# A decoder layer on one Trainium2 core: first rows by pairs, the 64-row products first, four shared lower parts behind the experts

## The chip, the cores and the metric

The kernel runs on one core of a Trainium2 chip. The metric is the device time of one execution in microseconds (us). Three runs of the kernel before gave 1570.51 to 1572.54 us, with a median of 1572.47 us. Beside them stands one execution that was recorded by the hardware profiler; every duration below is from it. A change of 0.2% is about 3.1 us.

## The reference, cut to what matters

Input `x` has 4 sequences of 512 rows of 512 numbers, all float32. Three blocks are each added to the running `x`:

```python
x = x + attention(layernorm(x), wq, wk, wv, wo)      # 32 query heads, 8 key/value heads, causal, rope
x = x + block_quantized(layernorm(x)) @ block_quantized(ctx).T
x = x + moe(layernorm(x))
# moe: probs = softmax(h @ Wg); every row goes to its best expert e (8 experts, 256 rows each at most);
#   routed = (silu(h @ W1[e]) * (h @ W3[e])) @ W2[e] * gate      # inner width 704 = 5 * 128 + 64
#   shared = (silu(h @ sw1) * (h @ sw3)) @ sw2                   # for all rows, inner width 704
#   x = x + routed + shared
```

## The kernel before, in words

**Order of work.** Every engine has one in-order stream of instructions, written out by the Python program. TensorE (PE) carries nearly all of the time. The program has four stages.

1. *The start* (lines 152 to 1056). The first sequence's four row tiles `h_0` to `h_3` (128 rows each) and the first weights are loaded. Two queues carry loads: `bulk` is ScalarE's (ACT's) queue, `nc.sync` is SyncE's (SP's). Meanwhile PE runs 52 transposes of the identity, `spin_a` (L169). VectorE (DVE) takes mean and variance of each row tile (`ln_mean_var`, L224 and L225), then an inverse root by an integer guess and three Newton steps on [128 x 4] values (`ln_root`, L238 to L247), then scales the four tiles (`ln_apply`, L251). PE transposes them (`ptr_h`, L257), ACT copies them into `hT` (L299), and PE goes on with the first value projection `psv` (L350; it needs only the first tile's part of `hT`), two transposes of the rope table `prt` (L1048) and the first key projection `psk` (L308; it needs all of `hT`).
2. *Attention.* A planner (`Fill`, with a due time, a cost and a chain of predecessors for each job) puts projections, output projections, the second block and the routing (`job_w`) between the score, transpose and value steps. The change leaves the order of this stage as it is.
3. *The shared expert, beside the last jobs* (`units`, from L1344). I write U(b,c) for `shared_up(b, c)`, the upper part of sequence b and inner chunk c, and D(b,j) for `shared_down(b, j)`, the lower part of the two row tiles j and j+1 of sequence b. Chunks 0 to 4 have 128 inner rows; chunk 5 holds the last 64. Except for b = 0, chunks 0 to 4 are computed by `up7` with seven half-size products instead of eight (L1281); it needs sums of blocks of the input, `xS`, made by `shared_sums(b)`, and of the weights, `wS`, made on GpSimd (POOL) by `weight_sums`. For the last sequence, b = 3, VectorE makes three of the four sums and POOL one. At the end of each chunk POOL multiplies the two halves into `gT` (L273). The order is U(0,0..5) D(0,0) U(1,5) D(0,2), U(1,0..4) D(1,0) U(2,5) D(1,2), U(2,0..4) D(2,0) U(3,5), U(3,0..4). The planner's last jobs run inside D(2,0): there the last sequence's routing product `pc` (L688), and from it, on DVE, the destinations `r_dst_i` (L712). Four indirect DMAs on POOL (L719) then scatter that sequence's rows into `xd`. Expert 0's two row tiles `xe` are read from `xd` by SP (L1397) and transposed on PE (`turn_rows(0)`, `ptr_e`) two units before the end of the stage, ahead of U(3,3).
4. *The experts and the tail.* For e = 0 to 7: five `up7` chunks of expert e (`p_e`), with expert e+1's weight sums on POOL; chunk 5 of expert e+1 (`expert_rest`); then the lower part `epy` (`down`, L1212 and L1222). `down` does two row tiles: for each, chunks 0 to 4 (two passes of a 128-row product each), and then for both the 64-row products of chunk 5 (L1222). Results go by VectorE (L1480) and SP (L1482) to `oe`. Behind expert 7 stand D(2,2), D(3,0) and D(3,2). Sixteen gathers on POOL (L1492) fetch the routed rows, VectorE adds them (`combine`, L1500), and SP writes the output (L1505, or L1341 where a shared lower part is added last). `rows_back` reads rows that had been parked in memory.

PSUM banks come from small rings: four named `sp`, three named `mm`, one `av`. A product that takes the next bank waits until its former content has been read.

Of the kernel before, what the change touches and what calls it, by code (L numbers as in the profile page):

```python
# [23 lines left out]
def decoder_layer(  # L24
# [92 lines left out]
    def tile_v(b):  # L117
        return pj.tile([P, KC, 512], F32, tag="wq", bufs=2, name=f"wv_{b}")

    def load_v(b):  # L120
        w = wts["v0"] if b == 0 else tile_v(b)
        bulk(out=w, in_=wv.rearrange("(k p) n -> p k n", p=P))
        wts["v"] = w

# [25 lines left out]
            issue(out=rows[b, j], in_=xf[i * P : (i + 1) * P, :])  # L150

    load_h(0)
    wts["v0"] = tile_v(0)
    load_v(0)
    load_k(0, 0)

    ident = const.tile([P, P], F32, name="ident")
# [2 lines left out]
    nc.gpsimd.tensor_copy(ident_b, ident)  # L160

    warm = const.tile([P, 1], F32, name="warm")
    nc.scalar.activation(warm, ident[:, 0:1], AF.Exp)

    def spin(n, name):

        pt = bank("sp", f"spin_{name}")
        for j in range(n):
            nc.tensor.transpose(pt[:, 0:P], ident, ident)  # L169

    spin(52, "a")

    mask = am1.tile([P, T], F32, name="mask")
    nc.gpsimd.memset(mask, 0.0)
# [155 lines left out]
    def job_k(b, a):  # L330

        t1 = yield from rotated(b, wts["k", a], 0, f"k_{b}_{a}")
        yield -0.6
        for g in range(2):
            kT = am1.tile([P, T], F32, tag="kT", bufs=4, name=f"kT_{b}_{2 * a + g}")
            for half in range(2):
                bulk(out=kT[half * HD : (half + 1) * HD, :], in_=t1[g * HD : (g + 1) * HD, :])
            kTs[b, 2 * a + g] = kT
# [692 lines left out]
    for _ in job_hs(0):  # L1031
        pass
    rsrc = am1.tile([P, TB, 2, 2, HD], F32, tag="pT", bufs=2, name="rsrc")
    for c in range(2):
        for half in range(2):
# [2 lines left out]
                rsrc[:, :, c, :, half * HH : (half + 1) * HH],  # L1038
                rp[:, :, c, lo : lo + HH].unsqueeze(2).to_broadcast([P, TB, 2, HH]),
            )  # L1040
    for gen in (job_h(0), job_v(0, 0)):
        for _ in gen:
            pass
    rt = pj.tile([P, 2, T], F32, name="rt")
    for c in range(2):
        pt = bank("mm", f"prt_{c}")
        for it in range(TB):
            nc.tensor.transpose(  # L1048
                pt[:, it * P : (it + 1) * P],
                rsrc[:, it, c, :, :].rearrange("p h d -> p (h d)"),  # L1050
                ident,
            )
        nc.scalar.copy(rt[:, c, :], pt)
    for gen in (job_k(0, 0), job_q(0, 0), job_q(0, 1), job_q(0, 2)):
        for _ in gen:
            pass
# [148 lines left out]
    def down(gT, w2, t, name, tag, mid=None):  # L1205

        pys = []
        for i in range(2):
            py = bank(tag, f"{name}_{i}")
            pys.append(py)  # L1210
            for c in range(HF):
                nc.tensor.matmul(  # L1212
                    py,
                    gT[:, c, (t + i) * P : (t + i + 1) * P],
                    w2[:, c, :],
                    start=(c == 0),
                    stop=False,
                )
                if mid and c % 2:
                    mid()  # L1220
        for i, py in enumerate(pys):
            nc.tensor.matmul(  # L1222
                py,
                gT[i * HT : (i + 1) * HT, HF, (t + i) * P : (t + i + 1) * P],
                w2[i * HT : (i + 1) * HT, HF, :],
                start=False,
                stop=True,
            )
        return pys

# [25 lines left out]
    def token_sums(x, ts, cols, vector=False):  # L1256

        half = cols // 2
        b11, b12, b21, b22 = (x[:, k : k + 2, t : t + half] for k in (0, 2) for t in (0, half))
        t1, t2, t3, t4 = ts  # L1260
        us = 1.27 * cols / T
        gpsimd(us, t3, b22, b12, ALU.subtract)
        for out, y, z in (t1, b12, b11), (t2, b22, t1), (t4, b21, t2):
            if vector:
                nc.vector.tensor_tensor(out, y, z, ALU.subtract)
            else:
                gpsimd(us, out, y, z, ALU.subtract)
        return t1, t2, t3, t4, b11, b21, b22
# [41 lines left out]
    def shared_up(b, c, mid=None):  # L1310
        if b not in gTs:
            gTs[b] = gp.tile([P, NHC, T], F32, tag="gT", bufs=2, name=f"gT_{b}")
        if b and c < HF:
            up7(se["w"][0], xS[b], gTs[b][:, c, :], c, T, f"s{b}_{c}", mid)
        else:
            up(se["w"][0], h3x[b], gTs[b], c, T, f"s{b}_{c}", mid)
        if not b and c < HF:
            weight_sums(se["w"][0], c)
            if c == 2:
                shared_sums(1)  # L1320
        if c == (HF - 1 if b else HF):
            se["next"] = b + 2
            load_h3(b + 2)
# [10 lines left out]
    def shared_down(b, j, mid=None):  # L1334
        for i in range(b * TB + j, b * TB + j + 2):
            xtile(i)
        for k, py in enumerate(down(gTs[b], se["w"][1], j, f"ys_{b}_{j}", "sp", mid)):
            i = b * TB + j + k
            nc.vector.tensor_tensor(xts[i], py, xts[i], ALU.add)
            if i in routed:  # L1340
                nc.sync.dma_start(out=outf[i * P : (i + 1) * P, :], in_=xts[i])  # L1341
            elif i not in kept:
                nc.sync.dma_start(out=x2[i * P : (i + 1) * P, :], in_=xts[i])
        if j == 0 and 0 < b < B - 1:  # L1344
            shared_sums(b + 1)

    kept = set()
# [35 lines left out]
    def load_w2(e):  # L1383
        if e < E:
            next(loads[e])
# [47 lines left out]

    ups = [u for u in units if u[0] is shared_up]
    downs = [u for u in units if u[0] is shared_down]
    units = [u for u in ups if u[2] == HF] + downs[:-3] + [u for u in ups if u[2] < HF]
    for i, (f, *args) in enumerate(units):
        if i == len(units) - 2:
            turn_rows(0)
            expert_sums(0)  # L1440
        rows_ahead(units[i + 1 :])
        f(*args)
        if f is shared_up and args[1] < HF:
            weight_sums(evw[0][0], args[1])
# [12 lines left out]
    def rows_back():  # L1457
        for i in first:
            xts[i] = spare.pop(0)
            nc.sync.dma_start(out=xts[i], in_=x2[i * P : (i + 1) * P, :])  # L1460
        for i in tiles[0] + tiles[1] + tiles[2]:
            xtile(i)

    for e in range(E):
        for c in range(HF):
            up7(evw[e][0], exS[e], egTs[e][:, c, :], c, CAP, f"e{e}_{c}")
            if e < E - 1:
                weight_sums(evw[e + 1][0], c)
            if c == 1:
                turn_rows(e + 1)  # L1470
                load_rows(e + 2)
            if c == 2:
                expert_sums(e + 1)
        expert_rest(e + 1)
        load_e(e + 2)
        if e == E - 1:
            rows_back()
        for t, py in enumerate(down(egTs[e], evw[e][1], 0, f"epy_{e}", "mm")):
# [4 lines left out]
        load_w2(e + 2)  # L1483

# [19 lines left out]
        if last:  # L1504
            nc.sync.dma_start(out=outf[i * P : (i + 1) * P, :], in_=xts[i])  # L1505

    for n, (f, *args) in enumerate(units):
        f(*args)
        if n == 0:
            for i in first + tiles[0] + tiles[2] + tiles[1]:  # L1510
                gather(i)
            for i in first + tiles[0]:
                combine(i, True)
        if n == 1:
            for i in tiles[2]:
                combine(i, False)
            for i in tiles[1]:
                combine(i, True)
    assert len(routed) == NT


# [58 lines left out]
```

## Time and profile before

| what | value |
|---|---|
| median of the three runs | 1572.47 us |
| the profiled execution's own time | 1569.79 us |
| its span (first to last instruction) | 1568.1 us |
| PE busy | 1530.8 us, 98% of the span |
| DVE, ACT, POOL busy | 920.8, 535.1 and 546.0 us |
| DMA moved | 194.42 MB, mean 124 GB/s |
| granted PE clock, mean | 0.998 |

The idle time of PE is the span less its busy time, some 37 us. By stretches of the span: 3.0 us of the first 40 us, 22.1 us of the next 1260 us (attention and the shared stage), 5.5 us of the 200 us from 1300 to 1500 us, 0.3 us of the next 40, and 6.3 us of the last 28 us. In a line of the timeline the columns are start and duration in us, engine, line, operation, output and inputs, shape, count, and in brackets the idle time just before and what ended it. In the list of waits a line has the waiter, the releaser, and then us in total, times, and the longest.

### The profile page before, as it was taken

Reading aid. Unit: us, or ns where it says so; the run is one execution under the profiler, and the core shown is the slowest. Engines: PE = TensorE matmul, PEld = TensorE weight load, DVE = VectorE, ACT = ScalarE, POOL = GpSimd, SP = SyncE. Lnnn points to the kernel's source line nnn. Section 1 sums busy time; section 2 is a strip of 40 time slices with the busy share of each in tenths; the row PEclk is TensorE's granted clock in tenths of the full one; section 3 lists DMA queues with packets and bytes.
Section 4 is the critical chain, followed back from the end, with each engine's and each line's share of the span. In section 5 each row is a group of like instructions: output and inputs, shape, how many; then the busy total and the mean of one; then the engine's idle time right before and its main releaser. Section 6 shows DMA issues by size and latency. Waiting matters only on the chain.

```text
span 1568.1 us, 22176 instructions
## 1 busy us (share of the span) xinstructions
PE 1530.8 (98%) x7324; PEld 890.5 (57%) x7324; DVE 920.8 (59%) x2732; ACT 535.1 (34%) x1611; POOL 546.0 (35%) x569
## 2 busy tenths in 40 slices
PE   9999999999999999999999999999999999999998
PEld 5455555455545545554555555555456867876873
DVE  4465843467776575887656495665665543443434
ACT  2354444334433434443444444452101221111110
POOL 2022301203334121334313133143445147776744
PEclk9999999999999999999999999999999999999999
DMA  4474430534234344423525342256051252655527
GB/s 142 129 222 148 101 101 21 158 105 102 79 84 142 88 123 140 102 88 75 146 84 133 118 114 61 61 159 191 19 210 54 81 193 76 208 178 184 191 90 260
DMA packets 118355, 194.42 MB, mean 124 GB/s; under 512 B 17120, under 2 KB 36576, under 8 KB 117728
## 3 DMA queue, kind: packets, MB, share of 16 engines
q10 hardware_dynamic: 65472, 100.94, 22.5%
q1 hardware_dynamic: 50208, 83.67, 17.6%
q0 software_dynamic: 2560, 8.39, 1.6%
q8 instruction: 58, 0.95, 0.3%
q14 instruction: 57, 0.47, 0.1%
HBM read 135.54 MB, written 28.05 MB: 104 GB/s over the span
## 4 chain that ended last, share of the span: by engine, by line
PE 69%; POOL 8%; DVE 2%; DMA 2%; issue 2%; ACT 1%; SPq 0%; ACTq 0%; POOLq 0%; DVEq 0%
PE py L408 12%; PE psq L308 10%; PE sc L939 7%; PE av L1020 7%; PE pt L989 6%; PE p_s L1281 5%; PE p_e L1281 5%; PE epy L1212 3%; PE p_s L1184 3%; PE psv L350 3%; POOL wS L273 3%; PE psk L308 3%; PE ys L1212 2%; POOL xS L273 1%; POOL slot_s L273 1%
## 5 line engine op out<-in xcount | busy, mean ns | idle before, releaser
L972 ACT ACTIVATE pm<-pm,mn 128x256 f32<-128x256 f32 (+3 forms) x512 | 281.0, 550 | 381.1 <-DVE mn L962 345.3
L962 DVE CUSTOM_DVE_ANT_0 pm<-sc,mask 128x256 f32<-128x256 f32 (+3 forms) x512 | 216.7, 485 | 91.4 <-PE sc L939 91.4
L408 PE MATMUL py<-wo,aT 128*128 128x512 f32 x512 | 239.2, 600 | 3.2 <-issue 2.0
L308 PE MATMUL psq<-hT,wq 128*128 128x512 f32 x512 | 236.5, 599 | 2.3 <-DVE y L604 2.3
L273 POOL TENSOR_TENSOR t1q<-t1q,tsq 128x512 f32<-128x512 f32 x64 | 83.9, 1312 | 391.1 <-DMA tsq<-t2q 154.1
L1006 DVE COPY pT<-pt 128x128 f32<-128x128 f32 (+3 forms) x256 | 114.2, 485 | 112.3 <-PE pt L989 104.0
L939 PE MATMUL sc<-kT,t1q 64*128 64x128 f32 (+3 forms) x1024 | 167.0, 451 | 6.8 <-ACT pT L1000 2.5
L989 PEld LDWEIGHTS pt<-ident,pm 128*128 128x128 f32 x1280 | 143.7, 141 | 36.2 <-issue 27.5
L989 PE MATMUL pt<-ident,pm 128*128 128x128 f32 x1280 | 154.4, 273 | 0.3 <-DVE mn L962 0.2
L1020 PE MATMUL av<-pT,v 128*64 128x512 f32 (+3 forms) x1024 | 152.3, 439 | 1.7 <-ACT pT L1000 1.7
L308 PEld LDWEIGHTS psq<-hT,wq 128*128 128x128 f32 x512 | 91.9, 190 | 102.1 <-issue 96.4
L1000 ACT COPY pT<-pt 128x128 f32<-128x128 f32 (+3 forms) x256 | 97.0, 430 | 147.6 <-PE pt L989 115.4
L408 PEld LDWEIGHTS py<-wo,aT 128*128 128x128 f32 x512 | 91.6, 190 | 97.8 <-issue 88.0
L939 PEld LDWEIGHTS sc<-kT,t1q 64*128 64x128 f32 x1024 | 86.4, 188 | 87.0 <-issue 58.3
L273 POOL TENSOR_TENSOR acc<-acc,y 128x512 f32<-128x512 f32 x64 | 81.0, 1270 | 153.3 <-DVE y L604 121.5
L1020 PEld LDWEIGHTS av<-pT,v 128*64 128x64 f32 x1024 | 68.3, 136 | 108.5 <-issue 96.4
L972 ACT ACTIVATION_READ_ACCUMULATOR pm<-pm,mn 128x1 f32 x512 | 95.7, 187 | 0.0
L273 POOL TENSOR_TENSOR aT<-aT,rrb 128x512 f32<-128x512 f32 x64 | 81.8, 1309 | 26.0 <-ACT pm L972 15.9
L1212 PE MATMUL epy<-slot_e,slot_s 128*128 128x512 f32 x160 | 71.8, 597 | 5.8 <-POOL slot_s L273 5.8
L1212 PE MATMUL ys<-slot_s,gT 128*128 128x512 f32 x160 | 71.7, 596 | 0.0
L416 DVE TENSOR_TENSOR acc<-py,acc 128x512 f32<-128x512 f32 x64 | 43.8, 686 | 46.3 <-PE py L408 45.6
L317 DVE TENSOR_TENSOR t2q<-psq,rt 128x512 f32<-128x512 f32 x64 | 44.0, 688 | 43.1 <-PE psq L308 40.2
(227 smaller groups left out, 2058.8 us busy)
## 6 DMA issues: line engine op xcount, KB each, us to landing
slot_e<-in_L_ffn_W_dram SPq DMA_DIRECT2D x14, 1280.0 KB
wq<-in_L_attn_wq_dram ACTq DMA_DIRECT2D x16, 1024.0 KB
tsq<-t2q SPq DMA_DIRECT2D x256, 64.0 KB
wo<-in_L_attn_wo_dram ACTq DMA_DIRECT2D x16, 1024.0 KB
rrb<-rrd ACTq DMA_DIRECT2D x32, 512.0 KB
slot_e<-in_L_ffn_W_dram SPq DMA_DIRECT2D x7, 1408.0 KB
kT<-t1k ACTq DMA_DIRECT2D x64, 128.0 KB
wv<-in_L_attn_wv_dram ACTq DMA_DIRECT2D x4, 1024.0 KB
```

The lines of the kernel that those rows point to most:

```text
L273: nc.gpsimd.tensor_tensor(*args)
L308: nc.tensor.matmul(ps, w[:, k, c0 : c0 + P], hTs[b][:, k, :], start=(k == 0), stop=(k == KC - 1),)
L408: nc.tensor.matmul(py, aT[:, r, j * P : (j + 1) * P], wts["o", a][:, r, :], start=(r == 0), stop=(r == 3),)
L939: nc.tensor.matmul(scs[g][:, o : o + nk], qTs[b, p][g * HD : (g + 1) * HD, it * P : nk], kTs[b, p // 2][g * HD : (g + 1) * HD, 0:nk], star ...
L962: nc.vector.tensor_tensor_reduce(out=pm[:, o : o + nk], in0=scs[g][:, o : o + nk], in1=mask[:, T - nk : T], scale=-(HD**-0.5), scalar=3.0e ...
L972: nc.scalar.activation(pm[:, o : o + nk], pm[:, o : o + nk], AF.Exp, bias=mn, scale=-1.0, accum_out=rss[b, a][:, col : col + 1],)
L989: nc.tensor.transpose(pt[:, j * P : (j + 1) * P], pms[g][:, j * P : (j + 1) * P], ident)
L1000: nc.scalar.copy(pT[:, 0 : it + 1, it * P : nk], pt[:, o : o + nk].rearrange("p (j t) -> p j t", t=P),)
L1006: nc.vector.tensor_copy(pT[:, it + 1, 0:nk], pt[:, o : o + nk])
L1020: nc.tensor.matmul(av[g * HD : (g + 1) * HD, j * P : T], vs[b][:, j, v0 : v0 + HD], rhs, start=(j == 0), stop=(j == TB - 1),)
L1212: nc.tensor.matmul(py, gT[:, c, (t + i) * P : (t + i + 1) * P], w2[:, c, :], start=(c == 0), stop=False,)
L1281: nc.tensor.matmul(ps, w[:, k, :], x[:, k, :], start=k == 0, stop=k == 1)
```

## The change

- `h_0` and `h_1` are normalized first, then `h_2` and `h_3`. ScalarE takes the root (table `Sqrt` loaded at the start instead of `Exp`), VectorE its reciprocal and one Newton step. PE's order becomes `ptr_h_0`, `ptr_h_1`, `psv`, `ptr_h_2`, `ptr_h_3`, `prt`, `psk`. `Exp` is loaded on ScalarE behind the `rt` copies. `wv` comes in halves, one on each queue, SP's half ahead of the rope table. `spin_a` has 41 transposes.
- `down` does the 64-row products of both row tiles first. For experts (`late`) chunk 4 of both row tiles is last.
- The four block sums are made in the order 1, 2, 3, 4. For b = 3 all four are VectorE's, and they stand right behind U(2,4).
- The order of units becomes U(2,0..4) U(3,5) U(3,0), with `pc` in the middle of U(3,5), then U(3,1..4), and D(2,0), D(2,2), D(3,0), D(3,2) behind expert 7. `turn_rows(0)` still stands ahead of U(3,3). On VectorE the steps from `r_cnt` (L698) to `gidx` (L717) come behind the fifth of U(3,0)'s seven reads of PSUM. On POOL the four scatters come ahead of U(3,0)'s product and of all of expert 0's weight sums.
- `rows_back` brings ten of the sixteen row tiles behind expert 5 and six behind expert 7's upper part. The gathers' order puts tiles of D(3,0) last.
- The very last lower part is `down_last`: row tile 2 whole, row tile 3 in two halves of 256 columns, each added and written as soon as it is done.

```diff
@@ the start
-    wts["v0"] = tile_v(0)
-    load_v(0)
+    wts["v"] = tile_v(0)
+    for k, issue in (0, bulk), (2, nc.sync.dma_start):
+        issue(out=wts["v"][:, k : k + 2, :],
+              in_=wv[k * P : (k + 2) * P, :].rearrange("(k p) n -> p k n", p=P))
...
-    nc.scalar.activation(warm, ident[:, 0:1], AF.Exp)
+    nc.scalar.activation(warm, ident[:, 0:1], AF.Sqrt)
...
-    spin(52, "a")
+    spin(41, "a")
...
+    def first_rows(js):
+        mv = mv0[:, js[0] : js[0] + 2, :]
+        for k, j in enumerate(js):
+            ln_mean_var(rows[0, j], mv[:, k, :], f"f{j}")
...
+        nc.scalar.activation(root, mv[:, :, 1], AF.Sqrt, bias=eps)
+        nc.vector.tensor_scalar(ve, mv[:, :, 1], LN_EPS, -0.5, ALU.add, ALU.mult)
+        nc.vector.reciprocal(rs, root)
+        nc.vector.tensor_tensor(r0, ve, rs, ALU.mult)
+        nc.vector.tensor_tensor(r0, r0, rs, ALU.mult)
+        nc.vector.scalar_tensor_tensor(rs, r0, 1.5, rs, ALU.add, ALU.mult)
+        for k, j in enumerate(js):
+            ln_apply(rows[0, j], rows[0, j], mv[:, k, :], rs[:, k : k + 1])
...
+    first_rows((0, 1))
+    turn = job_h(0)
+    for _ in range(2):
+        next(turn)
+    first_rows((2, 3))
...
-    for gen in (job_h(0), job_v(0, 0)):
+    for gen in (job_v(0, 0), turn):
...
+    nc.scalar.activation(warm, warm, AF.Exp)
@@ down: the 64-row products now open both banks (start=True) ahead of this loop
+        order = [(i, c) for i in range(2) for c in range(HF)]
+        if late:
+            order.sort(key=lambda x: x[1] == HF - 1)
+        for i, c in order:
+            nc.tensor.matmul(pys[i], gT[:, c, (t + i) * P : (t + i + 1) * P], w2[:, c, :],
+                             start=False, stop=(c == HF - 1))
+    def down_last(gT, w2, t, name):
+        parts = [(0, 0, D), (1, 0, D // 2), (1, D // 2, D)]
...
@@ token_sums
-        gpsimd(us, t3, b22, b12, ALU.subtract)
-        for out, y, z in (t1, b12, b11), (t2, b22, t1), (t4, b21, t2):
+        for out, y, z in (t1, b12, b11), (t2, b22, t1), (t3, b22, b12), (t4, b21, t2):
@@ shared_up, shared_down, units
+        if (b, c) == (B - 2, HF - 1):
+            shared_sums(B - 1)
...
-        if j == 0 and 0 < b < B - 1:
+        if j == 0 and 0 < b < B - 2:
             shared_sums(b + 1)
...
-            units.insert(-1, (shared_up, b + 1, HF))
+            units.insert(-1 if b < B - 2 else -2, (shared_up, b + 1, HF))
+        if b == B - 1:
+            units.insert(-8, units.pop(-7))
...
-    units = downs[-3:]
+    units = downs[-4:]
@@ experts and tail
         if e == E - 1:
-            rows_back()
+            rows_back(first[2:])
...
+        if e == E - 3:
+            rows_back(tiles[0] + first[:2])
...
+    for k, lo, hi, py in down_last(gTs[b], se["w"][1], j, f"ys_{b}_{j}"):
+        i = b * TB + j + k
+        nc.vector.tensor_tensor(xts[i][:, lo:hi], py, xts[i][:, lo:hi], ALU.add)
+        nc.sync.dma_start(out=outf[i * P : (i + 1) * P, lo:hi], in_=xts[i][:, lo:hi])
```

More of the change, by code (lines that the diff above doesn't have):

```diff
@@ L120, in load_v @@
     def load_v(b):
-        w = wts["v0"] if b == 0 else tile_v(b)
+        w = tile_v(b)
         bulk(out=w, in_=wv.rearrange("(k p) n -> p k n", p=P))
@@ L152, in decoder_layer @@
     load_h(0)
-    wts["v0"] = tile_v(0)
-    load_v(0)
+    wts["v"] = tile_v(0)
+    for k, issue in (0, bulk), (2, nc.sync.dma_start):
+        issue(
+            out=wts["v"][:, k : k + 2, :],
+            in_=wv[k * P : (k + 2) * P, :].rearrange("(k p) n -> p k n", p=P),
+        )
     load_k(0, 0)
@@ L162, in decoder_layer @@
     warm = const.tile([P, 1], F32, name="warm")
-    nc.scalar.activation(warm, ident[:, 0:1], AF.Exp)
+    nc.scalar.activation(warm, ident[:, 0:1], AF.Sqrt)
+    eps = const.tile([P, 1], F32, name="eps")
+    nc.vector.memset(eps, LN_EPS)
     def spin(n, name):
@@ L1029, in weighted, with t @@
         nc.scalar.copy(aTs[b, a][:, r, :], av)
-    for _ in job_hs(0):
-        pass
+    def first_rows(js):
+        mv = mv0[:, js[0] : js[0] + 2, :]
+        for k, j in enumerate(js):
+            ln_mean_var(rows[0, j], mv[:, k, :], f"f{j}")
+        def t(key):
+            return const.tile([P, TB], F32, tag=f"{key}a", bufs=2, name=f"{key}f_{js[0]}")
+        ve, r0, rs = (t(key) for key in ("ve", "r0", "rs"))
+        root, ve, r0, rs = ve[:, 2:4], ve[:, 0:2], r0[:, 0:2], rs[:, 0:2]
+        nc.scalar.activation(root, mv[:, :, 1], AF.Sqrt, bias=eps)
[6 more added lines that the diff above has]
+            ln_apply(rows[0, j], rows[0, j], mv[:, k, :], rs[:, k : k + 1])
+    mv0 = ln_tile("a", 0)
+    first_rows((0, 1))
[3 more added lines that the diff above has]
+    first_rows((2, 3))
     rsrc = am1.tile([P, TB, 2, 2, HD], F32, tag="pT", bufs=2, name="rsrc")
@@ L1203, in up, with down @@
         nc.vector.tensor_tensor(gv[HT:P, 1], pv[HT:P, 1], gv[HT:P, 1], ALU.mult)
[L1205 to L1220, printed above, removed]
+    def down(gT, w2, t, name, tag, mid=None, late=False):
+        pys = [bank(tag, f"{name}_{i}") for i in range(2)]
         for i, py in enumerate(pys):
@@ L1225, in down @@
                 w2[i * HT : (i + 1) * HT, HF, :],
+                start=True,
+                stop=False,
+            )
+        order = [(i, c) for i in range(2) for c in range(HF)]
+        if late:
+            order.sort(key=lambda x: x[1] == HF - 1)
+        for i, c in order:
+            nc.tensor.matmul(
+                pys[i],
+                gT[:, c, (t + i) * P : (t + i + 1) * P],
+                w2[:, c, :],
                 start=False,
-                stop=True,
+                stop=(c == HF - 1),
             )
-        return pys
+            if mid and c % 2:
+                mid()
+        return pys
+    def down_last(gT, w2, t, name):
+        parts = [(0, 0, D), (1, 0, D // 2), (1, D // 2, D)]
+        pys = [bank("sp", f"{name}_{n}")[:, 0 : hi - lo] for n, (i, lo, hi) in enumerate(parts)]
+        for py, (i, lo, hi) in zip(pys, parts):
+            nc.tensor.matmul(
+                py,
+                gT[i * HT : (i + 1) * HT, HF, (t + i) * P : (t + i + 1) * P],
+                w2[i * HT : (i + 1) * HT, HF, lo:hi],
+                start=True,
+                stop=False,
+            )
+        for py, (i, lo, hi) in zip(pys, parts):
+            for c in range(HF):
+                nc.tensor.matmul(
+                    py,
+                    gT[:, c, (t + i) * P : (t + i + 1) * P],
+                    w2[:, c, lo:hi],
+                    start=False,
+                    stop=(c == HF - 1),
+                )
+            yield i, lo, hi, py
     wS = gp.tile([P, 3, 2, HF * P], F32, name="wS")
@@ L1435, in decoder_layer @@
     downs = [u for u in units if u[0] is shared_down]
-    units = [u for u in ups if u[2] == HF] + downs[:-3] + [u for u in ups if u[2] < HF]
+    assert [u[2] for u in ups] == [*range(1, HF)] and len(downs) == 4
+    units = ups
     for i, (f, *args) in enumerate(units):
@@ L1441, in decoder_layer @@
         rows_ahead(units[i + 1 :])
+        if i == 0:
+            weight_sums(evw[0][0], 0)
         f(*args)
-        if f is shared_up and args[1] < HF:
-            weight_sums(evw[0][0], args[1])
+        weight_sums(evw[0][0], args[1])
     expert_rest(0)
-    units = downs[-3:]
+    units = downs[-4:]
     tiles = [[b * TB + j, b * TB + j + 1] for _, b, j in units]
@@ L1455, in decoder_layer, with rows_back @@
     spare += [wS_flat[:, k * D : (k + 1) * D] for k in range(NHC * CAP // D)]
-    def rows_back():
-        for i in first:
+    def rows_back(which):
+        for i in which:
             xts[i] = spare.pop(0)
             nc.sync.dma_start(out=xts[i], in_=x2[i * P : (i + 1) * P, :])
-        for i in tiles[0] + tiles[1] + tiles[2]:
-            xtile(i)
     for e in range(E):
@@ L1476, in decoder_layer @@
         if e == E - 1:
-            rows_back()
-        for t, py in enumerate(down(egTs[e], evw[e][1], 0, f"epy_{e}", "mm")):
+            rows_back(first[2:])
+        for t, py in enumerate(down(egTs[e], evw[e][1], 0, f"epy_{e}", "mm", late=True)):
             yo = ep.tile([P, D], F32, tag="yo", bufs=2, name=f"yo_{e}_{t}")
@@ L1483, in decoder_layer @@
         load_w2(e + 2)
+        if e == E - 3:
+            rows_back(tiles[0] + first[:2])
+            for i in tiles[1] + tiles[2] + tiles[3]:
+                xtile(i)
     ogs = {}
@@ L1505, in combine @@
             nc.sync.dma_start(out=outf[i * P : (i + 1) * P, :], in_=xts[i])
-    for n, (f, *args) in enumerate(units):
-        f(*args)
+    for n, (f, b, j) in enumerate(units[:-1]):
+        f(b, j)
         if n == 0:
-            for i in first + tiles[0] + tiles[2] + tiles[1]:
+            for i in first + tiles[0] + tiles[1] + tiles[3] + tiles[2]:
                 gather(i)
@@ L1514, in decoder_layer @@
         if n == 1:
-            for i in tiles[2]:
-                combine(i, False)
             for i in tiles[1]:
                 combine(i, True)
+            for i in tiles[3]:
+                combine(i, False)
+        if n == 2:
+            for i in tiles[2]:
+                combine(i, True)
+    _, b, j = units[-1]
+    for k, lo, hi, py in down_last(gTs[b], se["w"][1], j, f"ys_{b}_{j}"):
+        i = b * TB + j + k
+        nc.vector.tensor_tensor(xts[i][:, lo:hi], py, xts[i][:, lo:hi], ALU.add)
+        nc.sync.dma_start(out=outf[i * P : (i + 1) * P, lo:hi], in_=xts[i][:, lo:hi])
     assert len(routed) == NT
```

## The prediction

> **What bounds the kernel now.** First I read the page's busy times: PE works 1530.8 of 1568.1 us. No product goes, apart from eleven warming transposes, so only PE's idle 37 us can be won, and new waits can be added to it. Next I read PE's waits.
>
> ```profile
> PE epy L1212 <- POOL slot_s L273: 5.8, 7, 0.8
> PE p_s L1281 <- DVE xt L1339: 2.6, 1, 2.6
> PE p_s L1281 <- POOL xS L273: 1.4, 1, 1.4
> ```
>
> The first is an expert's lower part waiting for POOL's product of chunk 4, seven times; the third is the shared stage waiting for the block sums of b = 3. The second lies in U(1,0) at 1164 us, behind a normalization on DVE that the change does not touch. Then I read the timeline at the four places that the change edits. The start, the experts (experts 0 and 7), the last sequence's rows, and the end:
>
> ```profile
> 10.46 2.09 DVE L251 TENSOR_SCALAR h<-h,mva,rsa 128x512 f32<-128x512 f32 x4
> 11.08 2.24 PE L257 MATMUL ptr_h<-ident,h 128*128 128x128 f32 x16 [1.36 <-DVE h L251]
> ...
> 17.47 3.67 PE L308 MATMUL psk<-hT,wk 128*128 128x512 f32 x8
> ```
> ```profile
> 1320.86 3.60 PE L1212 MATMUL epy<-slot_e,slot_s 128*128 128x512 f32 x8
> 1325.29 5.42 PE L1212 MATMUL epy<-slot_e,slot_s 128*128 128x512 f32 x12 [0.83 <-POOL slot_s L273]
> 1330.63 1.13 PE L1222 MATMUL epy<-slot_e,slot_s 64*128 64x512 f32 x4
> ...
> 1522.40 8.75 PE L1212 MATMUL epy<-slot_e,slot_s 128*128 128x512 f32 x20
> 1531.08 1.13 PE L1222 MATMUL epy<-slot_e,slot_s 64*128 64x512 f32 x4
> ```
> ```profile
> 1259.54 1.01 POOL L719 DMA_INDIRECT xd<-h,r_dst_i  x1 [1.36 <-DVE r_flat L715]
> ...
> 1272.16 0.80 SPq L1397 DMA_DIRECT2D xe<-xd  x2
> ...
> 1287.93 1.04 PE L257 MATMUL ptr_e<-ident,xe 128*128 128x128 f32 x8
> ```
> ```profile
> 1560.60 1.13 PE L1222 MATMUL ys<-slot_s,gT 64*128 64x512 f32 x4
> ...
> 1563.53 1.28 DVE L1339 TENSOR_TENSOR xt<-ys,xt 128x512 f32<-128x512 f32 x2
> ```
>
> See: PE stands idle for `h_0`; expert 0's lower part takes 9.77 us to its 64-row products and expert 7's, which waits for nothing, 8.68; expert 0's rows are asked for at 1272 us and used at 1288, so they have 16 us; and PE is done at 1561.73 us, 6.4 us ahead of the end.
>
> **The start: 2.1 us won.** The variance of `h_1` is done at 6.22 us (timeline of DVE). Behind it now stand one small ACT operation (0.20 us, row of `warm`), a reciprocal (0.18 us) and three small steps at the 0.2 us pace of the Newton rows: 1.1 us. So `h_0` is scaled from 7.35 to 7.9 us instead of from 10.46. That is not last: the spin is. It runs at some 5 per us up to 6.5 us and at some 10 per us after (starts per half microsecond), so eleven fewer end it 1.1 us earlier, at about 8.6 us. From there: two tiles' transposes at 0.49 us each to 9.6; `hT`'s first part at 9.9 (0.70 from transpose to copy, 0.54 for the copy); `psv` 3.45 us, to 13.35 (32 like it in the trace start 0.43 apart); the other two tiles to 14.35; `prt` 0.87 us; `psk` at 15.3 us instead of 17.44. DVE has `h_2` and `h_3` by 12.3 us, hidden under `psv`. The DMAs run full at about 360 GB/s from 3 to 13 us. `wv`'s halves now move side by side and should land by 8.5 us, by bytes at that rate; the rope table, which landed at 10.0, waits for half of `wv` and should land at 10.5 to 11, and with POOL's 1.8 us is ready 1 us ahead of `prt`. The table load on ACT (1.28 us) lies where ACT has nothing to do until the first softmax. If the first tile's transposes wait for the root, the gain is 1 us; with a faster spin it is 3.
>
> **D(0,0): 1.6 us lost.** It stands right behind U(0,5), which makes the 64 rows. Their chain in this place is PE's end at 1134.0 us, ACT's Silu 1134.12 to 1134.71, and DVE's two products from 1135.07 and 1135.51 (behind routing steps). Before, it lay under D(0,0)'s twenty 128-row products; now these rows are first, and PE waits from 1134.0 to 1135.6. Bounds: 1.2, if DVE were free at once, and 2.0, if the second product counts in full. The jobs behind it hang on PE, so it isn't won back. Every other lower part has its 64 rows done one unit or more ahead.
>
> **The block sums of b = 3: 1.6 us won.** U(3,0) takes 7.68 us (1268.17 to 1275.85) and U(3,1) 6.04. The sums waited for D(2,0)'s results, POOL's one for the scatters. Now they follow U(2,4)'s last read of PSUM, at 1255.6, four at 0.69 us, with 3.5 us of U(3,5) beside them. Their input `h3x` was issued at 1247.22, and the DMA share falls to nothing at 1251.5, so it is there.
>
> **Expert 0's rows: 3.5 us lost.** D(2,0), some 10 us, goes from between `pc` and `ptr_e`, and the 1.6 us with it, so PE reaches `ptr_e` at 1276.3 us in this clock. The rows come later: U(3,0) starts at 1258.1 (1254.22 plus 3.53 of U(3,5) plus 0.37 of `pc`), the fifth read of PSUM ends 4.9 us after a unit's start (rows of U(3,1)), the steps from `r_cnt` to `r_dst_i` take 1.5 us without the 1.1 us for which one of them stood beside a POOL operation, and 0.3 later the first scatter starts: 1264.8 instead of 1259.54. The scatters are serial, each waiting for the one before. The request for `xe` came 12.6 us after the first, so now at 1277.4, or 0.6 earlier if the third scatter isn't slowed as it was while rows were written (3.58 us against 3.0). The DMA share rises 0.9 us after the request, and by the bytes `xe_0` is there 2.2 to 2.5 us after it: 1279.1 to 1279.9. PE waits 2.8 to 3.6 us, and 0.3 for the second tile. I take 3.5; the bounds are 0, if the rows come as in D(2,0)'s days, and 5.8, if each of the four serial steps lost the 0.6 us that the third did.
>
> A wait of this length meets the clock. The profile has one case: at 352.9 us PE, after 2.3 us of transposes, stood idle for 1.46 us, and the granted clock was 0.5 from 354.5 to 357.5 us; after the 2.58 us in U(1,0) it stayed at 1.00. Here 3.5 us idle are followed by 0.9 us of transposes. If the gate closes, 3 us at half speed cost 1.5 us. I leave that out of the sum and keep it as a case. [...] In the trace the gap of 2.58 us behind full products is free, and one of 1.46 us behind transposes isn't.
>
> **The experts: 7.6 us won.** 9.77 less 8.68 is 1.09 us, and the seven lower parts with the wait take 9.75 to 9.79 each. Now chunk 4 is read 1.06 us (64 rows) plus 16 products of 0.43 after the start, 7.9 us, while POOL's product was ready 4.4 us after it. What is late next is chunk 3, read 3.6 us after the start and ready 0.6 after it. POOL's order is unchanged. In expert 0 it starts 2.4 us later against PE, since the scatters run longer, and has slack. Bounds: 5.8, the list's idle time alone, and 7.6.
>
> **The end: 2.6 us won.** Four lower parts of 9.84 us (1532.14 to 1541.98) instead of three bring nothing by themselves: it is the one taken from the middle. But the sixteen gathers, 20 us on POOL, then end some 10 us ahead of PE. Before, the last gathered rows held DVE until 1563.6, so the last additions ran 1.8 us behind PE. Now there is one addition of 128 x 256 behind PE (0.42 us by `up7`'s rows, 0.1 to start). From the last addition (1564.81) to the end of the span were 3.3 us. So 3.8 instead of 6.4. Its output is half as large: up to 0.4 more. DVE's additions for D(3,0) stand behind gathered rows of tiles 14 and 15 and hold a bank that `down_last` needs; they should come 1 us ahead of it. If the gathers land 2 us later, 1 us is lost.
>
> **Sum:** -2.1 + 1.6 - 1.6 + 3.5 - 7.6 - 2.6 = -8.8 us. The profiled execution took 1569.79 us (1.7 outside of the span), so 1561.0. The median of the runs is 2.7 above it; I carry the difference over: 1572.5 - 8.8 = 1563.7 us.
>
> **Rivals.**
> - *Rows in time* (0.13): the scatters and reads gain on PE, the 3.5 us go: 1560.2. For it, spacings of 3.0; against it, four serial trips to memory.
> - *The clock gate closes* behind that wait for 3 us: 1565.2 (0.22).
> - *POOL's product stays last* (0.09): the experts' wait only moves to an earlier chunk, the 7.6 us are not won: 1571.3. Against it stand 3 us of slack in chunk 3.
> - *Slower* (0.06): the gate closes at `ptr_e` and stays closed into U(3,3), U(3,4) and expert 0. Half of the time at half clock is lost, so from 12 us lost, 24 us closed, it is slower by over 0.2% (8.8 to lose, and 3.1). Closed for 30 us it gives 1578.7. For it: these units keep PE at it with short products and small pauses; against it: the trace's one case lasted 3 us.
>
> **The numbers.** The forecast has 0.50. Measurement here tells some 0.2%, 3.1 us, from no change: under 1569.3 us is faster. That holds for forecast, rows in time and clock gate: 0.85. POOL staying last is the same: 0.09. Slower: 0.06. For the range the bounded terms (start 1 us either way, D(0,0) 0.4, rows from 3.5 less to 2.3 more, experts up to 1.8 less, end 1, runs 1) are laid around the forecast, with both cases of the rows: 1558.5 to 1569.0. Left out are POOL staying last and slower, 0.15.
>
> **What would show it.** Right: `psk` at 15 us; a wait of 1.6 us of the first `ys` 64-row products on DVE at about 1132; no `epy` wait on POOL; a wait of `ptr_e` on the DMA of `xe` of 3 to 4 us; one small addition behind PE's end. Wrong would be the sum if PE waits for `wv` or the rope table, if the gate closes, or if DVE holds banks in the last two lower parts.

## The result, and the profile after

Six runs of the changed kernel took 1562.72 to 1567.81 us, with a median of 1564.03. Six runs of the kernel before beside them had a median of 1571.49. The ratio is 0.9956 (95% interval 0.9944 to 0.9968), 7 us. The forecast was 1563.7. The rival *the clock gate closes* stood at 1565.2, so the median alone does not choose between the two.

The two profiled executions differ by less: 1567.81 us after, 1569.79 before. The first part of the page says where to look. PE's idle time, span less busy time, fell from 37.3 to 31.1 us (1566.1 less 1535.0), but PE's *busy* time rose by 4.2 us, with eleven transposes fewer. And the mean granted clock fell from 0.998 to 0.993.

First the waits. The view lists who waited for whom: engine, tile and line, releaser, then us in total, times, longest. After:

```profile
PE ptr_e L263 <- DMA xe<-xd: 3.2, 1, 3.2
PE p_s L1336 <- DVE xt L1396: 3.1, 1, 3.1
...
PE ys L1242 <- DVE gT L1234: 1.5, 1, 1.5
```

The second line is U(1,0)'s wait, 3.1 us where it was 2.6. `epy` and `xS`, the first and the last of the three lines shown before, are not in the list. The new waits, for expert 0's rows (first) and at D(0,0) (last), have the predicted place and length. Next the timeline of PE, at the start and in expert 0's lower part:

```profile
8.21 1.04 PE L263 MATMUL ptr_h<-ident,h 128*128 128x128 f32 x8
...
14.90 3.63 PE L314 MATMUL psk<-hT,wk 128*128 128x512 f32 x8
```
```profile
1319.66 1.13 PE L1242 MATMUL epy<-slot_e,slot_s 64*128 64x512 f32 x4
1320.72 8.85 PE L1253 MATMUL epy<-slot_e,slot_s 128*128 128x512 f32 x20
1329.41 0.61 PE L1336 MATMUL p_e<-h3x,slot_e 128*128 128x128 f32 x4
```

`psk` starts 2.6 us earlier than before. The lower part runs from 1319.66 to 1329.41 without a bracket: 9.75 us, where 9.77 were needed before to reach the 64-row products and 1.1 more for these. Then the path of expert 0's rows (the first and the last of four scatters, the request, the transposes), and the end:

```profile
1268.93 1.01 POOL L725 DMA_INDIRECT xd<-h,r_dst_i  x1 [6.07 <-DVE r_flat L721]
...
1277.78 0.96 POOL L725 DMA_INDIRECT xd<-h,r_dst_i  x1 [1.97 <-DVE u_s L1346]
1280.84 0.80 SPq L1457 DMA_DIRECT2D xe<-xd  x2
...
1283.85 1.94 PE L263 MATMUL ptr_e<-ident,xe 128*128 128x128 f32 x8 [3.21 <-DMA xe<-xd]
```
```profile
1553.99 8.88 PE L1278 MATMUL ys<-slot_s,gT 128*128 128x512 f32 x30
...
1562.91 0.42 DVE L1590 TENSOR_TENSOR xt<-ys,xt 128x256 f32<-128x256 f32 x1 [1.73 <-PE ys L1278]
```

From PE's end (1562.87) to the end of the span are 3.2 us, where there were 6.4. And the eight transposes of `ptr_e` take 1.94 us; before, the same eight took 1.04.

That is the clock. The table by stretches of 3.4 us has PE's busy time, the other engines', the granted clock (PEclk), and the DMA share. Around `ptr_e`, after:

```profile
core 0: us, PE busy (x) PEld busy (x) DVE busy (x) ACT busy (x) POOL busy (x), PEclk, DMA share, GB/s
1275.80:1279.20 3.40, 3.40 (x18) 2.99 (x17) 1.27 (x3) 0.13 (x1) 1.41 (x3) 1.00 0.19 77
1279.20:1282.60 3.40, 1.45 (x7) 0.94 (x5) 1.42 (x4) 0.75 (x2) 3.17 (x5) 1.00 0.41 122
1282.60:1286.00 3.40, 2.15 (x9) 2.10 (x10) 0.00 (x0) 0.76 (x2) 3.24 (x5) 0.51 0.94 320
1286.00:1289.40 3.40, 3.40 (x9) 2.70 (x8) 0.09 (x1) 0.79 (x2) 3.30 (x4) 0.50 1.01 375
```

In the second stretch PE is busy for 1.45 us; in the third and fourth it has half the clock. In the fourth it is busy throughout and gets nine products done where the first has eighteen. So the wait of 3.2 us costs some 6: half of the 5.55 us that PE is busy in the third and fourth is 2.8 more. Between 50 us and the last two microseconds the trace has four more such stretches, of 3.4 us each, at 354, 586, 1136 and 1167 us. That of before has one, from 354.55 to 357.96 us, also 3.4 us long, where the prediction has 3.

**Two sums.** To keep work and clock apart I use one quantity for all kernels below. In all fourteen traces the granted clock is 1.0 or 0.5, and in the table above PE gets nine products done at 0.5 where it gets eighteen at 1.0. So with a mean granted clock c over a span S, a time of 2(1-c)S ran at half speed, and (1-c)S was lost, if PE was the limit (an upper bound: a PE that stands idle loses nothing). Time less this loss I call *time at full clock*. The clock is given to three digits, 0.8 us for one run, so it takes the mean of several. Within the kernels a run's time follows its loss (correlation 0.71, slope 0.73, 139 runs). With 0.73 of the loss taken off instead of all of it, the 8.9 us below would be 8.5.

| kernel | runs | median us | before beside it | ratio, 95% interval | lost to the clock | at full clock |
|---|---|---|---|---|---|---|
| before, three batches | 51 | 1570.89 to 1572.69 | | | 4.5 | 1567.1 |
| changed, first runs and once more | 12 | 1564.03, 1563.03 | 1571.49, 1571.59 | 0.9956, 0.9948 | 6.0 | 1558.2 |
| e1, rows a unit later | 5 | 1557.72 | 1571.59 | 0.9912 (0.9899 to 0.9924) | 2.5 | 1555.2 |
| e2, D(0,0)'s 64 rows last | 5 | 1559.97 | 1571.59 | 0.9928 (0.9915 to 0.9941) | 4.1 | 1555.9 |
| e3, experts' old order | 11 | 1572.85 | 1570.89 | 1.0009 (0.9999 to 1.0019) | 6.0 | 1566.0 |
| e4, seven products as filling | 5 | 1565.12 | 1571.59 | 0.9953 (0.9940 to 0.9966) | 3.4 | 1561.0 |
| e5, old start | 11 | 1569.20 | 1570.89 | 0.9986 (0.9977 to 0.9994) | 6.8 | 1562.1 |
| e6, before and the experts' new order | 6 | 1563.48 | 1570.89 | 0.9946 (0.9930 to 0.9961) | 3.4 | 1559.2 |
| e7, D(2,0) not moved | 11 | 1569.69 | 1570.89 | 0.9990 (0.9981 to 0.9998) | 7.0 | 1562.6 |
| e8, three products as filling | 6 | 1561.34 | 1572.69 | 0.9929 (0.9914 to 0.9945) | 3.9 | 1558.0 |
| e9, e1 and e2 together | 4 | 1554.33 | 1572.69 | 0.9879 (0.9864 to 0.9893) | 1.9 | 1552.9 |
| e10, D(2,0) not moved, no halves | 6 | 1560.45 | 1572.69 | 0.9921 (0.9909 to 0.9933) | 2.9 | 1557.8 |
| e11, no halves at the end | 6 | 1565.38 | 1572.69 | 0.9945 (0.9928 to 0.9962) | 6.5 | 1558.0 |

The last column is good to some 0.5 us (standard errors 0.2 to 0.8). At full clock the change won 8.9 us; the prediction's sum was 8.8. The clock took back 1.5.

### The profile page after: what moved, and what is told of

Read it like the earlier page. It is cut to its first block, busy times and chain, and to the rows that moved or that the text cites. A ratio compares the mean times of both kernels' runs of the same rounds, so it can differ in the third digit from the quotient of the medians.

```text
span 1566.1 us, 22168 instructions
## 1 busy us (share of the span) xinstructions
PE 1535.0 (98%) x7325; PEld 895.8 (57%) x7325; DVE 920.8 (59%) x2732; ACT 537.4 (34%) x1615; POOL 544.9 (35%) x568
## 4 chain that ended last, share of the span: by engine, by line
PE 86%; DVE 4%; DMA 3%; issue 2%; ACT 2%; POOL 2%; SPq 0%; ACTq 0%; POOLq 0%; DVEq 0%
PE py L414 14%; PE psq L314 13%; PE sc L945 9%; PE av L1026 8%; PE p_e L1336 8%; PE pt L995 8%; PE p_s L1336 5%; PE epy L1253 4%; PE psv L356 4%; PE ys L1253 4%; PE psk L314 3%; ACT pm L978 1%; PE p_s L1216 1%; PE p_e L1216 1%; PE ptr_h L263 1%
## 5 line engine op out<-in xcount | busy, mean ns | idle before, releaser
L945 PE MATMUL sc<-kT,t1q 64*128 64x384 f32 (+3 forms) x1024 | 166.7, 450 | 7.3 <-ACT pT L1006 2.5
L1253 PE MATMUL ys<-slot_s,gT 128*128 128x512 f32 x140 | 64.4, 610 | 0.0
```

Source lines behind the costliest of these rows:

```text
L945: nc.tensor.matmul(scs[g][:, o : o + nk], qTs[b, p][g * HD : (g + 1) * HD, it * P : nk], kTs[b, p // 2][g * HD : (g + 1) * HD, 0:nk], star ...
L1253: nc.tensor.matmul(pys[i], gT[:, c, (t + i) * P : (t + i + 1) * P], w2[:, c, :], start=False, stop=(c == HF - 1),)
```

## The experiments

Theory: the six terms of the prediction hold as they stand, and the clock behind the two new waits takes a part of the gain back. Rivals: the gain comes from fewer of the terms than that, a wait costs only its own length, and the move of D(2,0) pays.

**The changed kernel again (e0).** No edit.

> The changed kernel itself once more, beside the three experiments of its batch. Its profiled run took 1567.8 us with five stretches at half clock, while four of its six runs took 1562.7 to 1564.3. If the difference is the clock gate (theory), a profile of a faster run has fewer or shorter stretches at half clock, by 2 to 4 us of lost time, and the instructions' waits (ptr_e 3.2 us, first products of D(0,0) 1.5 us, U(1,0) 3.1 us) stay. If it is something else (rival: DMAs or jobs that fall otherwise), the stretches stay and the waits differ. Median 1563 to 1565 us.

Measured: 1559.80 to 1567.78 us, median 1563.03. The runs with a clock of 0.998 took 1559.8 and 1562.0, those with 0.995 took 1565.9 and 1567.8. The profiled run (1564.05) has the same waits (`ptr_e` 3.3 us, U(1,0) 3.1) and half clock behind 50 us in three places (354, 1163, 1279 us) instead of five. The theory stands: these two profiles of one kernel differ by where the clock falls, not by what waits.

**Expert 0's rows a unit later (e1).**

```diff
-        if i == len(units) - 2:
+        if i == len(units) - 1:
             turn_rows(0)
             expert_sums(0)
...
-            exS[e] = token_sums(xTs[e], ts, CAP)
+            exS[e] = token_sums(xTs[e], ts, CAP, e == 0)
```

> The changed kernel with expert 0's rows turned ahead of U(3,4) instead of U(3,3), and its token sums on VectorE. Theory: the 3.2 us wait of ptr_e for the DMA and the half clock behind it (6.4 us long in the profile) are the price of moving D(2,0); both go, so 3 to 6 us less than the changed kernel: 1558 to 1561 us. Rival 1, the wait alone costs: 3 us less. Rival 2, PE's wait only moves, to expert 0's first products that wait for the token sums or to the pointwise chain of U(3,4): 0 to 1 us less.

Measured: 1557.72 us, 5.3 less than the changed kernel beside it. At full clock 3.0 less, the wait; lost to the clock 3.5 less. Its timeline of PE, at the transposes:

```profile
1282.61 1.04 PE L263 MATMUL ptr_e<-ident,xe 128*128 128x128 f32 x8
```

No bracket, and 1.04 us for the transposes. Both parts of the theory's price, wait and clock, are there and go together; the two rivals fall.

**D(0,0)'s 64-row products last (e2).** In `down` the products of chunk 5 come behind the others again, for D(0,0) alone; the first and the last product of each bank carry `start` and `stop`.

```diff
+        order = order + rest if rest_last else rest + order
...
-down(gTs[b], se["w"][1], j, f"ys_{b}_{j}", "sp", mid)
+down(gTs[b], se["w"][1], j, f"ys_{b}_{j}", "sp", mid, rest_last=(b, j) == (0, 0))
```

> The changed kernel with the 64-row products of D(0,0) alone put back behind the 128-row ones. Theory: the 1.5 us wait there goes, and the half clock behind it (3.4 us long in the profile, some 1.7 us lost), where it had closed: 1.5 to 3.2 us less than the changed kernel, 1561 to 1562.5 us. Rival: the jobs behind it give it back, since U(1,0) waits for a normalization on VectorE, which would then just be longer (3.1 us plus what PE gained): 0 us less, 1564.

Measured: 1559.97 us, 3.1 less than the changed kernel. The start of D(0,0) in its timeline has no wait:

```profile
1128.78 6.17 PE L1248 MATMUL ys<-slot_s,gT 128*128 128x512 f32 x14
```

2.3 us are won at full clock and 1.9 on the clock. U(1,0) still waits 3.1 us for VectorE, not longer, so the jobs behind did not give it back. The theory holds.

**Filling the wait (e4, then e8).** Unread products are put ahead of expert 0's transposes, so that PE works where it would wait. Seven of them in e4; e8 has `range(3)`.

```diff
         if i == len(units) - 2:
+            fill = bank("mm", "fill")
+            for _ in range(7):
+                nc.tensor.matmul(fill, h3x[B - 1][:, 0, 0:P], h3x[B - 1][:, 0, :], start=True, stop=True)
             turn_rows(0)
```

> The changed kernel with seven products of 128x128 by 128x512 that nothing reads, some 3.0 us of PE's time, put ahead of expert 0's transposes, where PE waits 3.2 us for rows. Nothing that is used comes earlier by it. Theory: half of the price there is the clock that falls after the idle time; with PE kept at work the granted clock stays at 1.0 through ptr_e and U(3,3), and the kernel is 1.5 to 2.9 us faster than the changed one, though it does more work: 1561 to 1562.5 us. Rival: only the wait counts, the products fill it and nothing is won: 1564 us; if the clock falls all the same, 1564 to 1565.

Measured: 1565.12 us, no gain. My size was wrong: a product of this shape is two passes (the three of e8 stand in its timeline as x6, 2.74 us), and seven take 6.0 us, 0.86 each. They outlast the wait by 2.8 us, which is the 2.8 us that e4 is slower at full clock; it loses 2.6 us less to the clock. So gain and price cancelled, and e8 does it with the right size.

> The changed kernel with three unread products (128x128 by 128x512) instead of seven ahead of expert 0's transposes. In the run with seven the granted clock stayed at 1.00 there, but each of them took 0.86 us, twice what I had reckoned, so that they filled 6.0 us where PE waits 3.3, and won nothing. Three take 2.6 us, less than the wait. Theory: the half clock behind the wait (one or two steps of 3.41 us, 1.7 to 2.9 us lost) goes and nothing is added: 1.5 to 3 us less than the changed kernel, 1561 to 1562.5. Rival: the price at ptr_e is the wait alone: 1564, and what a closed clock costs is hidden under the engines behind PE.

Measured: 0.9929, against 0.9948 and 0.9956 for the changed kernel: 3 to 4 us less, though the intervals overlap. At full clock nothing changes (-0.2); the clock's loss is 2.1 us smaller (standard error 0.9). The table of stretches of e8 shows it better than the times (columns PE's busy time, granted clock, DMA):

```profile
1275.20:1278.70 3.50, 3.50 (x15) 1.00 0.21 83
1278.70:1282.10 3.40, 2.69 (x15) 1.00 0.82 255
1282.10:1285.50 3.40, 3.40 (x18) 1.00 1.00 348
```

The rows come no earlier (0.7 us of the wait are left), but the clock stays at 1.00 behind the transposes, and PE gets eighteen products done in the last stretch. So work that nobody reads most likely made the kernel faster: by this table, and by the smaller loss in e4 and e8, the price at `ptr_e` was not the wait alone.

**The experts' old order (e3) and the new order alone (e6).**

```diff
-down(egTs[e], evw[e][1], 0, f"epy_{e}", "mm", late=True)     # the changed kernel
+down(egTs[e], evw[e][1], 0, f"epy_{e}", "mm", rest_last=True)   # e3: chunks 0 to 4, then the 64 rows
...
-down(egTs[e], evw[e][1], 0, f"epy_{e}", "mm")                # the kernel before
+down(egTs[e], evw[e][1], 0, f"epy_{e}", "mm", late=True)        # e6: 64 rows, chunks 0 to 3, then 4
```

> The changed kernel with the experts' lower parts in the order of before (128-row products of chunks 0 to 4 for both row tiles, the 64 rows last). Theory: seven waits of 1.09 us for GpSimd's product of chunk 4 come back, 7.6 us more than the changed kernel: 1570 to 1571.5 us. Rival, POOL's wait only moved to another chunk or to the next unit: 0 to 3 us more.

> The kernel before with one edit, the experts' lower parts in the new order (64 rows first, chunk 4 of both row tiles last). Theory: it wins its 7.6 us alone, 1563.5 to 1564.5 us, as much as the whole change nets, since the rest of the change (start and end won, rows and D(0,0) lost, with half clock behind them) cancels to about nothing. Rival, a part of the gain needs D(2,0) moved or the earlier rows: 3 us or less, 1568 to 1569.

Measured: e3 takes 1572.85 us, 7.8 more than the changed kernel at full clock. Its wait is back in each of the seven lower parts, as here in expert 0's:

```profile
1315.75 3.60 PE L1248 MATMUL epy<-slot_e,slot_s 128*128 128x512 f32 x8
1320.10 6.48 PE L1248 MATMUL epy<-slot_e,slot_s 128*128 128x512 f32 x16 [0.76 <-POOL slot_s L279]
```

e6 takes 1563.48 us, 0.9946 of before, 7.9 less at full clock. One edit in the order of twelve products brings as much as the whole change. All the rest of it, in these runs, cancelled.

**The old start (e5).** The start of the kernel before, with its 52 transposes, its `ln_root` over four tiles, and one load of `wv`; the rest as changed.

```diff
-    spin(41, "a")
+    spin(52, "a")
...
-    first_rows((0, 1))
...
+    for _ in job_hs(0):
+        pass
```

> The changed kernel with the start of before (four rows normalized together, VectorE's root, 52 warming transposes, one load of wv). Theory: the start is worth 2.1 to 2.6 us, as the first sc stands 2.6 us earlier in the profile: 1565 to 1566 us. Rival, the attention stage's waits on ScalarE and VectorE take it back before 370 us, as the lead shrinks to 0.7 to 1.1 us by then: 1 us or less, 1563 to 1564.

Measured: 1569.20 us, 5 more than the changed kernel, twice what I expected: 3.9 at full clock, and 0.8 on the clock. The table of stretches shows what I had missed, first in e5, then in the kernel before:

```profile
8.30:11.70 3.40, 1.26 (x11) 0.94 (x9) 3.06 (x14) 0.00 (x0) 1.57 (x4) 1.00 1.11 337
11.70:15.10 3.40, 3.40 (x15) 2.88 (x14) 0.97 (x2) 2.34 (x4) 0.24 (x1) 0.52 0.53 195
```
```profile
8.30:11.70 3.40, 2.04 (x19) 1.69 (x17) 3.06 (x14) 0.00 (x0) 1.69 (x4) 1.00 1.11 341
11.70:15.10 3.40, 3.40 (x18) 2.20 (x18) 0.85 (x2) 2.17 (x4) 0.12 (x1) 1.00 0.53 194
```

Where the old spin ends a little earlier, PE is busy for 1.26 us instead of 2.04 of the stretch ahead of `ptr_h`, and the next one runs at half clock. Then the first `sc` stands at 32.98 us (e6, with the same start, 32.91), against 31.37 in the profile before and 28.77 after. The new start leaves no such gap. So in these profiles it is worth 2.6 us where the old start keeps its clock, and 4.2 where it doesn't. The 0.8 us that e5 loses more to the clock fit that, with a standard error of 1.0; at full clock 1.3 us (standard error 0.7) over the 2.6 remain, and I have not found their place.

**D(2,0) left where it was (e7, e10), and the end without halves (e11).** e7 takes the units' order, block sums, rows and gathers of before, and keeps the new start, all of `down` and `down_last`. e10 is e7 without `down_last`. e11 is the changed kernel without `down_last`:

```diff
-    for n, (f, b, j) in enumerate(units[:-1]):
+    for n, (f, b, j) in enumerate(units):
         f(b, j)
...
-    _, b, j = units[-1]
-    for k, lo, hi, py in down_last(gTs[b], se["w"][1], j, f"ys_{b}_{j}"):
...
```

> The changed kernel without the move of D(2,0): the units, block sums, three lower parts behind the experts and the gathers of before, with the new start, the new order in all lower parts and the last lower part by halves. Theory: the rows come in time (no wait and no half clock at ptr_e, 5 to 6 us won), but the block sums' wait of 1.4 us and 2 us of the end come back: 2 to 3 us less than the changed kernel, 1560.5 to 1562. Rival, the move pays: 1 to 3 us more than the changed kernel.

Measured: 1569.69 us, 4.3 more than the changed kernel at full clock and 1.0 on the clock. My expectation was wrong. The rows are in time, as expected, but the timeline of PE has a new wait at the end:

```profile
1547.06 1.12 PE L1269 MATMUL ys<-slot_s,gT 64*128 64x512 f32 x4
1552.92 1.22 PE L1269 MATMUL ys<-slot_s,gT 64*128 64x256 f32 x2 [4.74 <-DVE xt L1395]
```

`down_last` opens three banks of a ring of four, and two are still held by D(3,0), whose additions stand on VectorE behind gathered rows that have not come. Behind these 4.7 us PE ran at half clock as well, from 1551.2 to 1558.0 us.

> The changed kernel without the move of D(2,0) and without the last lower part by halves. With halves and without the move, PE stood 4.7 us for the banks that VectorE held behind the gathers, and two steps of half clock followed. Theory: that collision was what made that kernel 6 us slower than the changed one, so without the halves it goes: the end and the block sums cost 3.1 + 1.4 us more than in the changed kernel, the rows and their half clock 5 to 6 us less, 1562 to 1564 us. Rival, the move pays by itself: 1566 or more.

Measured: 1560.45 us, below the 1562 to 1564 that I expected; the ratio, 0.9921, is 4 to 5.5 us under the changed kernel's 0.9948 and 0.9956. At full clock it equals the changed kernel (1557.8, 1558.2); it loses 3.1 us less to the clock, and its profile has no wait at `ptr_e`. So the collision of halves and late gathers was e7's fault, and the move of D(2,0) with `down_last` wins nothing: by these sums its gains at the end and in the block sums pay for the rows' wait, and the clock behind that wait is the net loss.

> The changed kernel with D(2,0) moved, but its last lower part computed like the others instead of by halves. Theory: the end's gain is the gathers' head start, which the fourth lower part gives, and the halves are worth only the size of the last addition and output, 0.3 to 0.8 us: 1564 to 1565. Rival, the halves carry the end's gain: 2 to 3 us more than the changed kernel, 1566 to 1567.

Measured: 0.9945; at full clock 0.2 us from the changed kernel, within the error. By the times, the halves are worth less than can be told here. The profiles divide the end: from PE's end to the end of the span are 6.4 us before, 5.0 in e10, 3.9 in e11 and 3.2 after. So the halves shorten it by some 0.6 us, and the head start of the gathers by 1.1 us (e10 to e11) to 2.5 (before to e11). And the profile of e11 has a case that the times alone can't give: PE waited 3.3 us at `ptr_e` and the clock did not fall.

```profile
1278.90:1282.30 3.40, 1.12 (x6) 1.00 0.44 125
1282.30:1285.70 3.40, 2.33 (x15) 1.00 0.91 307
```

These stretches are not laid on the clock's own steps (below). On those, PE was busy for 1.43 us in the one that begins at 1279 us and for 2.06 in the next. The same wait fell on the edge.

**Both mendings (e9).** The edits of e1 and e2.

> The changed kernel with both mendings, expert 0's rows ahead of U(3,4) with its token sums on VectorE, and the 64-row products of D(0,0) alone behind the 128-row ones. Theory: the two lost terms are independent, so their gains add, 5.3 and 3.1 us: 1555 to 1556.5 us, about 1% under the kernel before. Rival, part of each was the same luck with the clock's steps: 5 to 6 us less, 1558.

Measured: 1554.33 us, 0.9879 of the kernel before (0.9864 to 0.9893), some 11 us under the changed kernel. At full clock 5.3 us less than it: 3.0 and 2.3, added. The clock's loss is 1.9 us (standard error 1.2) instead of 6.0. Two of its four runs took 1553.2 us with a clock of 1.000 as listed. It is the fastest kernel of the study. e10 with e2's edit was not run.

## Why the prediction was right, point by point

- **The start, -2.1: right, a little small.** 2.6 us at `psk` and still at the first `sc`; taking it out (e5) cost 3.9 at full clock, and 1.3 of that are open. The spin did end last (8.4 us, predicted 8.6). `psk` came at 14.90, not 15.3, since the transposes began at 8.21, not 8.6. Not seen: the old start lost its clock at 12 us in two of its three profiles (e5, e6; not before), the new one in none of eleven.
- **D(0,0), +1.6: right for the wait,** 1.5 us on DVE at the predicted place; e2 gives 2.3 for its removal at full clock. Missed: its clock. The wait is short, and I did not think of it as a case; but the step with it held 1.58 to 2.07 us of work in five profiles (after, e3, e5, e7, e11), and the next ran at half clock; with 1.92 to 1.96 us in e1, e8 and e10 it did not.
- **Block sums, -1.6: right.** The wait for `xS` is gone from the list. It was undone only together with the move (e7, e10), so it has no measured price of its own.
- **Expert 0's rows, +3.5: right, 3.2 us** in the profile and 3.0 by e1. The scatters came 2.95 us apart, and the rows 3 us after the request (SP 1280.84, first transpose 1283.85), where I had 2.2 to 2.5.
- **The experts, -7.6: right.** 7.8 by taking it out, 7.9 by putting it in alone. This one term is as large as the whole net gain.
- **The end, -2.6: 3.2** from PE's end. But my reason mixed two edits: the gathers' head start carries most of it (2.5 us from before to e11), and the halves, whose smaller output I gave up to 0.4, bring 0.6 in the profiles and nothing that the times can tell.
- **U(1,0), put at nothing: wrong.** Its wait, "behind a normalization on DVE that the change does not touch", rose by some 0.5 us. The order in `down` touches it. By the timelines, D(0,2)'s 64-row products, 1.1 us, stood between its last job and U(1,0), and now stand ahead of the jobs, so PE comes sooner to the bank that VectorE still holds. All twelve profiles with the new order there wait 3.0 to 3.1 us, and the clock fell behind each; before and e6, whose shared lower parts keep the old order, wait 2.6, and it did not fall:

```profile
PE p_s L1275 <- DVE xt L1333: 2.6, 1, 2.6
```

- **The sum, -8.8: measured -8.9 at full clock.** What failed is the line below it, "I leave that out of the sum and keep it as a case": the clock did fall behind `ptr_e` in most profiles of kernels with that wait (after, e0, e2, e3, e5; not e11), for one or two steps. The rival *the clock gate closes* put +1.5 us on the sum, and the loss rose from 4.5 us before to 6.0 after. That the two agree is luck: without the wait at `ptr_e` the loss is 3.5 us smaller (e1), without that at D(0,0) 1.9 (e2), and without both it is 1.9 us in all (e9), less than before. That the forecast's 1563.7 was met all the same is luck too: the kernel before ran at 1571.5 in the later runs, 1 us under the median that I had started from: 1571.5 - 8.9 + 1.5 = 1564.1.
- The other rivals: *rows in time* fell, *POOL's product stays last* fell (e3, e6), *slower* fell: the clock came back within 6.8 us each time.

The case for which I had least evidence, one closing behind 1.46 us of idle time and none behind 2.58, was the informative one. The length of the gap alone did not tell the two apart; what did in part is in the last section.

## What to carry to other kernels

In this kernel, with PE busy for 98% of the span, a new wait cost its length and, by chance of where it fell, up to two steps (3.4 us each) of half clock behind it: for the 3.1 to 3.4 us at `ptr_e`, two in after, e0 and e5, one in e2 and e3, none in e11. So of two orders with equal sums take the one without the wait, or fill it with work that costs less than the wait. Look at PE's busy time between two profiles: where it rises though work was taken away (here by 4.2 us), divide it into stretches with the granted clock before looking for contention. And take a bundle of edits apart: here one order of twelve products gave as much as the whole, the gains of the other parts were given back, and one of them (`down_last`) costs 5 us at full clock, and some 10 with the clock, as soon as the part that covers it is left out (e7 against e10).

## What the runs showed of the hardware

**In these traces the clock moves in steps of 3.413 us.** In all fourteen every stretch of granted clock between two changes is a whole multiple of 3.413 us (in the profile after, the 228.7 us from 357.65 to 586.35 us are 67 of them), counted from an origin that differs from run to run against the kernel's first instruction: a step begins at 0.22 us in e1, at 2.67 in after, at 2.98 in before and at 3.36 in e8. The best measure I found is PE's busy time within one such step. Between 14 and 1550 us, among steps at full clock: 21 had PE busy for up to 1.42 us, and all 21 were followed by a step at half clock; over 6100 had more than 2.1 us, and none was; of the 58 between, 14 were. Between these bounds busy time alone does not decide. Of the nine steps near 350 us with 1.95 us of work, mostly transposes, eight were followed by half clock; of ten near 1067 us with 1.64 to 1.72 us, none was. What else counts is open. A step at half clock led to a second one when PE was busy in it for 2.2, 2.2, 2.4 and 2.7 us (after, e0, e5, e4), and not at 2.7 (e2) and more. So the gap of 2.6 us that lay across two steps in before did nothing (U(1,0): 1.51 us busy in its emptier step, clock 1.00), and one of 3.0 to 3.1 us there was followed by half clock in each of the twelve profiles that have it. It need not be: two of e9's runs list a clock of 1.000, which leaves less than 0.8 us lost in the whole run, and one step loses 1.7. Six runs of the changed kernel spread by 5 and by 8 us; that the origin of the steps sets which gaps count is what the traces suggest for it, but only one run of each kernel has a trace.

**VectorE beside GpSimd.** In the profile after, at 1259.7 to 1263.4 us, three of the block sums of b = 3 take 0.68 to 0.69 us and the fourth, which overlaps a GpSimd product of 1.70 us, takes 1.75. The third overlaps the first 0.6 us of that GpSimd product and is no longer than the others; the product itself takes 1.27 to 1.28 us in the places where it meets none of the sums. So 1.1 us hung here on which operations of the two engines met, and in which order; it was hidden, and it is one case.
